# A mark for weights of ones on the softmax sums, with a simpler order of the loop

## The chip, the cores and the metric

The kernel runs on one core of a Trainium2 chip. The metric is the device time of one execution, in microseconds. The core's engines have a queue of instructions each and wait for one another by semaphores: TensorE (PE in the profile, its weight loads PEld), VectorE (DVE), ScalarE (ACT), GpSimd (POOL), and SyncE (SP), which issues most of the transfers.

## What is computed

A block of three layers on x of shape (2, 256, 128, 128), that is batch, time, bands, channels, all in float32: attention over time with a causal mask, attention over the bands with a mask of |i - j| <= 16, and a feed-forward layer, each after a layer norm and each added to its input. There are 4 heads of 32 channels.

```
xt = _ln(x, ln_t_w, ln_t_b).transpose(0, 2, 1, 3)
x = x + _mha(xt, t_wi, t_bi, t_wo, t_bo, H_T, cm).transpose(0, 2, 1, 3)
xf = _ln(x, ln_f_w, ln_f_b)
x = x + _mha(xf, f_wi, f_bi, f_wo, f_bo, H_F, bm)
xn = _ln(x, ln_n_w, ln_n_b)
h = jax.nn.gelu(xn @ w1.T + b1, approximate=False)
x = x + (h @ w2.T + b2)
```

In `_mha` the scores are `q k / sqrt(32)` plus the mask, `attn` their softmax over the keys, and the output `(attn v) wo.T + bo`.

## The kernel before

The work is cut into 384 groups of 512 rows of 128 channels, NT = 4 tiles of 128 rows. First come 128 groups of attention over time (`OverTime`, two sequences of 256 steps each), then 32 rounds of four groups of attention over bands (`OverBands`, four sequences of 128 bands each) and four feed-forward groups (`FeedForward`) on the same rows. The class `Attention` holds what the two attentions share.

A group goes through stages, each a method that emits the instructions of one step:

- `load` issues the transfer of the input (for several groups at once).
- `statistics` makes mean and variance on VectorE (`stats`, `mv`) and 1/sqrt on GpSimd (`rstd`, two instructions).
- `normalize` makes `xh` on VectorE, four instructions.
- `transpose` has four transposes on TensorE into `xp`, and `take_transposed` copies them to `xnT` on VectorE.
- `queries_keys` and `values` are the projections `qp`, `kp` and `vp`; `take_query`, `take_key` and `take_values` copy them out, on ScalarE but for the key over time, which VectorE takes.
- `first_half` and `second_half` make scores `sp` on TensorE, each head on 32 rows of the array; `first_function` and `second_function` take their exponential on ScalarE (`pt`, `pf`) and clear what the mask excludes, on GpSimd, and for head 3 over bands by a product with a band of ones on VectorE.
- `weigh` sums the weights over the keys by a product with ones (`rp`, each head's sums on its own 32 columns of the array) and multiplies them with the values (`op`). There is no maximum taken out: a test at the start of the program shows that the scores are small enough.
- `invert` makes 1/rp on ScalarE as exp(-ln(rp)), and `divide` refines it and divides on VectorE: `t`, `u`, `oT`. `divide_alone` does the same with VectorE's reciprocal.
- `bias` adds the output's bias to the residual, on GpSimd.
- `output` is the last projection `yp`, and `finish` adds it to the residual on VectorE and issues the store, where there is one.

A feed-forward group uses the same names: its halves are two hidden products `hp` each, its functions two GELUs into `hT`, its `weigh` the second product `zp` and its `divide` the addition to the residual and the store.

Every engine keeps the order in which the program emits (`keep_in_program_order`), so the loop in `run` (lines 878 to 923) sets the order of all five engines by hand. Step n emits the scores of group n, the weighing of group n - 1, and the projections of group n + 1. `near(n, far, name)` calls a stage for a group 2 ahead if it is attention and 1 ahead if it is feed-forward (`AHEAD`), with `far` more. The loop before has three orders: one for the first feed-forward group after bands (all hidden products at once, `divide_alone`), one for the second, and one for all else. In it the output of group n - 2 stands at the start of step n, all four heads' scores over bands are made in `first_half`, and the transposes of a feed-forward group come ahead of the second pair of hidden products.

ScalarE needs one table of functions for exp and ln and another for GELU, so the loop changes tables twice a round. All PSUM tiles come from one pool of eight banks, taken in turn. All products are float32 on both sides.

In the profile nearly all lines are L798, that of the helper `pinned` that emits; groups are told apart by tile names.

Of the kernel before, what the change touches and what calls it, by code (L numbers as in the profile page):

```python
# [9 lines left out]
F32 = mybir.dt.float32  # L10
# [3 lines left out]
ALU = mybir.AluOpType  # L14
# [4 lines left out]
P = 128  # L19
H = 4  # L20
D = 32
# [3 lines left out]
NT = 4  # L25
# [4 lines left out]
EXP_SET = "natural_log_exp_and_others"  # L30
# [393 lines left out]
class Group:  # L424
# [58 lines left out]
    def second_half(self):  # L483
        pass

    def second_function(self):
        pass
# [32 lines left out]
class Attention(Group):  # L520
# [57 lines left out]
        self.oT = path.work.tile([P, NT * P], F32, name="oT", bufs=2)  # L578
        vector.scalar_tensor_tensor(self.oT, t, 2.0, u, ALU.subtract, ALU.mult)

    def divide_alone(self):

        path, vector = self.path, self.path.vector
        r = path.work.tile([P, NT * P], F32, name="r", bufs=2)
        vector.reciprocal(r, self.rp)
        self.oT = path.work.tile([P, NT * P], F32, name="oT", bufs=2)
        vector.scalar_tensor_tensor(self.oT, self.op, -1.0, r, ALU.mult, ALU.mult)

    def output(self):
        path = self.path  # L590
        self.yp = path.bank([P, NT, P], "yp")
# [11 lines left out]
def rows_of(h):  # L603
    return slice(h * D, (h + 1) * D)


class OverTime(Attention):
# [4 lines left out]
    W = 3 * P  # L612
# [45 lines left out]
    def weigh(self):  # L658
        path = self.path
        p, v, W = self.p, self.v, self.W  # L660
        rp = path.bank([P, 2, 2 * P], "rp")
        one = path.k.ones[:, 0:D]
        for h in range(H):
            path.tensor.matmul(rp[rows_of(h), :, :], one, p[:, :, h, 0 : 2 * P], start=True, stop=False)
        for h in range(H):
            path.tensor.matmul(rp[rows_of(h), :, P : 2 * P], one, p[:, :, h, 2 * P : W], start=False, stop=True)
        op = path.bank([P, 2, 2 * P], "op")
        for s in range(2):
            for h in range(H):
                r = rows_of(h)  # L670
                path.tensor.matmul(op[r, s, :], v[:, 2 * s, r], p[:, s, h, 0 : 2 * P], start=True, stop=False)
            for h in range(H):
                r = rows_of(h)
                path.tensor.matmul(
                    op[r, s, P : 2 * P], v[:, 2 * s + 1, r], p[:, s, h, 2 * P : W], start=False, stop=True
                )
        self.op = op.rearrange("p s q -> p (s q)")
        self.rp = rp.rearrange("p s q -> p (s q)")


class OverBands(Attention):
# [32 lines left out]

    def first_half(self):
        self.p = self.path.work.tile([P, H, NT, P], F32, name="pf", tag="p")
        self.scores(range(H))

    def first_function(self):
        self.weights(range(H))  # L720

    def weigh(self):
        path = self.path
        self.rp = path.bank([P, NT * P], "rp")
        for h in range(H):
            path.tensor.matmul(
                self.rp[rows_of(h), :], path.k.ones[:, 0:D], self.p[:, h].rearrange("p i q -> p (i q)"),
                start=True, stop=True,
            )
        self.op = path.bank([P, NT * P], "op")  # L730
        for i in range(NT):
            c = slice(i * P, (i + 1) * P)
            for h in range(H):
                r = rows_of(h)
                path.tensor.matmul(self.op[r, c], self.v[:, i, r], self.p[:, h, i, :], start=True, stop=True)
# [67 lines left out]
class BoundedPath:  # L803
# [19 lines left out]
    def bank(self, shape, name):  # L823
        return self.ps.tile(shape, F32, name=name, tag="ps")

    def groups(self, x, out):
        nc, k = self.nc, self.k
        B, T, FB, C = x.shape
        NC_T = T // P
        S = NT // NC_T  # L830
        for b in range(B):
            xv = x[b].rearrange("(o p) f c -> p o f c", p=P)
            x1v = k.x1[b].rearrange("(o p) f c -> p o f c", p=P)
            for f0 in range(0, FB, GA):
                held = {}

                def load(f0=f0, xv=xv, held=held):
                    held["x"] = self.xpool.tile([P, GA, NC_T, C], F32, name="xt", tag="x")
                    for o in range(NC_T):
                        nc.sync.dma_start(held["x"][:, :, o, :], xv[:, o, f0 : f0 + GA, :])  # L840

                for g in range(0, GA, S):

                    def src(g=g, held=held):
                        return held["x"][:, g : g + S].rearrange("p f o c -> p (f o) c")

                    def store(t, f=f0 + g, x1v=x1v):
                        for o in range(NC_T):
                            nc.sync.dma_start(
                                x1v[:, o, f : f + S, :],  # L850
                                t.rearrange("p (f o) c -> p f o c", o=NC_T)[:, :, o, :],
                            )

                    yield OverTime(self, src, None, load if g == 0 else None, store)
        for b in range(B):
            x1v = k.x1[b].rearrange("t f c -> f t c")
            outv = out[b].rearrange("t f c -> f t c")
            for t0 in range(0, T, GB):
                held = {}

                def load(t0=t0, x1v=x1v, held=held):
                    held["x"] = self.xpool.tile([P, GB, C], F32, name="xb", tag="x")
                    nc.sync.dma_start(held["x"], x1v[:, t0 : t0 + GB, :])
                    held["x2"] = self.xpool.tile([P, GB, C], F32, name="x2", tag="x2", bufs=2)

                def part(name, g, held=held):
                    return lambda: held[name][:, g : g + NT, :]

                for g in range(0, GB, NT):
                    yield OverBands(self, part("x", g), part("x2", g), load if g == 0 else None)  # L870
                for g in range(0, GB, NT):

                    def store(t, g=t0 + g, outv=outv):
                        nc.sync.dma_start(outv[:, g : g + NT, :], t)

                    yield FeedForward(self, part("x2", g), None, None, store)

    def run(self, x, out):
        groups = list(self.groups(x, out))

        def do(n, *names):
            if 0 <= n < len(groups):
                for name in names:
                    getattr(groups[n], name)()

        def near(n, far, name):

            for d in (1, 2):
                if 0 <= n + d + far < len(groups) and groups[n + d + far].AHEAD == d:
                    do(n + d + far, name)  # L890

        def at(n, kind):
            return 0 <= n < len(groups) and isinstance(groups[n], kind)

        def move(n):
            near(n, 0, "transpose")
            near(n, 0, "take_transposed")

        self.scalar.preload_act_table_set(EXP_SET)
        for n in range(-7, len(groups) + 2):  # L900
            feeding = [at(n - i, FeedForward) for i in range(3)]
            do(n + 7, "load")
            near(n, 0, "normalize")
            if feeding[0] and at(n - 1, OverBands):

                do(n, "first_half", "first_function", "second_half", "second_function")
                do(n - 2, "output", "finish")
                near(n, 1, "statistics")
                move(n)
                do(n, "bias")  # L910
                do(n - 1, "weigh", "divide_alone")
            elif feeding[1] and at(n - 2, OverBands):
                do(n, "first_half", "first_function", "bias")
                do(n - 1, "weigh", "divide")
                move(n)
                do(n - 2, "output", "finish")
                near(n, 1, "statistics")
                do(n, "second_half", "second_function")
            else:
                do(n - 2, "output", "finish")  # L920
                near(n, 1, "statistics")
                if feeding[1] and at(n, OverBands):
                    self.scalar.preload_act_table_set(EXP_SET)
                do(n, "first_half", "first_function", "bias")
                early = at(n, OverBands) and at(n + 1, FeedForward)
                if early:
                    move(n)
                do(n - 1, "weigh", "invert", "divide")
                if feeding[0] and at(n + 1, FeedForward):
                    move(n)  # L930
                    early = True
                do(n, "second_half", "second_function")
                do(n + 1, "queries_keys", "take_query", "take_key", "values", "take_values")
                if not early:
                    move(n)


def bounded_path(tc, k, x, out):
# [66 lines left out]
```

## Time and profile before

| | us |
|---|---|
| median of 3 runs | 3130.95 (3130.63 to 3132.49) |
| the profiled execution | 3130.63 |
| its span, first to last instruction | 3128.7 |
| a step of the stage over time (128 of them) | 8.59 |
| a round of four band and four feed-forward groups (32) | 62.2 |

Granted clock of TensorE: 0.999 in the profiled execution. The stage over time takes the first 1,140 us or so of the span, and the rounds take the rest. In one round TensorE is busy 59.4 us, VectorE 45.6, GpSimd 37.4 and ScalarE 32.4. A product's time in the profile is that of its record, which overlaps the next one's; what it costs TensorE is the distance from its start to the start of the next.

### The profile page before, as it was taken

What the parts mean: (1) busy time and instruction counts of PE and PEld (TensorE: products, weight loads), DVE (VectorE), ACT (ScalarE), POOL (GpSimd) and SP (SyncE); (2) the same over time, 40 slices, a digit from 0 to 9 for tenths busy, and PEclk for the clock granted to TensorE, in tenths of its full rate; (3) what the DMA queues carried; (4) which work ended last, traced back from release to release, by engine and by line L of the source; (5) the groups of instructions that cost most, each with busy time, mean ns of one, the idle gap of its engine ahead of it and who ended that gap; (6) DMA issues with size and microseconds to landing.
All of it is one profiled execution on the core that took longest, in us unless ns stands there. A gap on an engine that the chain in (4) does not pass through costs nothing.

```text
span 3128.7 us, 77496 instructions
## 1 busy us (share of the span) xinstructions
PE 3013.3 (96%) x31270; PEld 2133.5 (68%) x31270; DVE 2246.7 (72%) x6414; ACT 1748.6 (56%) x3200; POOL 1889.3 (60%) x2441
## 2 busy tenths in 40 slices
PE   7999999999999999999999999999999999999998
PEld 5666666666666666666666666666666666776676
DVE  6776767777677677677767767776777677767775
ACT  4666666666666664554455445544554555455544
POOL 4666666666666665566556656665665566556654
PEclk9999999999999999999999999999999999999999
DMA  3222222222222221101111111111101110111000
GB/s 84 59 59 72 59 59 60 71 59 61 72 61 59 59 62 35 35 28 43 34 35 28 45 35 32 28 45 35 32 28 45 35 32 28 45 35 32 28 22 22
DMA packets 222863, 140.55 MB, mean 45 GB/s; under 512 B 7968, under 2 KB 205984, under 8 KB 222496
## 3 DMA queue, kind: packets, MB, share of 16 engines
q1 hardware_dynamic: 221248, 134.45, 15.3%
q8 instruction: 249, 4.08, 0.5%
q10 hardware_dynamic: 1248, 1.05, 0.1%
q14 instruction: 118, 0.97, 0.1%
HBM read 68.36 MB, written 67.11 MB: 43 GB/s over the span
## 4 chain that ended last, share of the span: by engine, by line
PE 80%; DVE 13%; ACT 5%; issue 1%; DMA 0%; POOL 0%; SPq 0%; ACTq 0%; POOLq 0%; DVEq 0%
PE zp L798 15%; PE hp L798 15%; PE sp L798 10%; PE yp L798 7%; PE rp L798 7%; PE qp L798 6%; PE op L798 6%; PE vp L798 5%; PE kp L798 5%; PE xp L798 4%; DVE xh L798 3%; ACT pf L798 3%; DVE stats L798 2%; DVE oT L798 2%; DVE t L798 1%; DVE x L798 1%
## 5 line engine op out<-in xcount | busy, mean ns | idle before, releaser
L798 POOL TENSOR_SCALAR rstd<-mv 128x4 f32<-128x4 f32 x384 | 99.2, 258 | 1131.9 <-DVE mv L798 1131.9
L798 ACT ACTIVATE hT<-hp,b 128x512 f32<-128x512 f32 x512 | 351.9, 687 | 620.8 <-PE hp L798 616.4
L798 ACT ACTIVATE pt<-sp 128x384 f32<-128x384 f32 x1024 | 419.3, 496 | 303.6 <-PE sp L798 303.6
L798 POOL TENSOR_SCALAR_AFFINE_SELECT pf<-pf 128x512 f32<-128x512 f32 x768 | 533.9, 711 | 38.6 <-ACT pf L798 12.3
L798 PEld LDWEIGHTS zp<-w2T_sb,hT 128*128 128x128 f32 x4096 | 475.0, 192 | 50.4 <-issue 38.7
L798 PE MATMUL hp<-xnT,w1f 128*128 128x512 f32 x1024 | 471.5, 598 | 34.0 <-DVE xnT L798 34.0
L798 PE MATMUL zp<-w2T_sb,hT 128*128 128x128 f32 x4096 | 481.5, 276 | 0.1
L798 DVE COPY xnT<-xp 128x512 f32<-128x512 f32 x384 | 260.0, 684 | 278.9 <-PE xp L798 278.9
L798 POOL TENSOR_TENSOR rstd<-rstd,mhalf 128x4 f32<-128x4 f32 x384 | 399.7, 1041 | 32.0
L798 PE MATMUL sp<-qT,kT 32*128 32x128 f32 (+1 forms) x8192 | 389.4, 315 | 0.0
L798 ACT ACTIVATE pf<-sp 128x512 f32<-128x512 f32 x512 | 264.4, 602 | 202.9 <-PE sp L798 202.6
L798 PEld LDWEIGHTS sp<-qT,kT 32*128 32x128 f32 x8192 | 310.8, 185 | 64.6 <-issue 35.9
L798 PEld LDWEIGHTS vp<-wf,xnT 128*128 128x128 f32 x2048 | 269.1, 192 | 123.0 <-issue 85.5
L798 PEld LDWEIGHTS hp<-xnT,w1f 128*128 128x128 f32 x1024 | 181.9, 190 | 218.6 <-issue 162.4
L798 PE MATMUL yp<-wn,oT 128*128 128x128 f32 x2048 | 275.1, 277 | 46.8 <-DVE oT L798 46.8
L798 POOL TENSOR_SCALAR_AFFINE_SELECT pt<-pt 128x512 f32<-128x512 f32 x512 | 314.4, 636 | 0.0
L798 PEld LDWEIGHTS yp<-wn,oT 128*128 128x128 f32 x2048 | 251.1, 192 | 73.9 <-ACT v L798 58.6
L798 PE MATMUL qp<-xnT,wf 128*128 128x512 f32 x512 | 282.7, 634 | 1.2 <-DVE xnT L798 1.2
L798 DVE TENSOR_TENSOR t<-rp,r 128x512 f32<-128x512 f32 x224 | 154.5, 690 | 174.8 <-ACT r L798 173.9
L798 PE MATMUL vp<-wf,xnT 128*128 128x128 f32 x2048 | 269.9, 275 | 0.0
L798 DVE TENSOR_SCALAR xh<-x,mv,rstd 128x128 f32<-128x128 f32 x512 | 256.3, 562 | 15.1 <-POOL rstd L798 15.1
L798 PE MATMUL kp<-xnT,wf 128*128 128x512 f32 x512 | 262.3, 594 | 0.0
(94 smaller groups left out, 4630.5 us busy)
## 6 DMA issues: line engine op xcount, KB each, us to landing
xt<-in_x SPq DMA_DIRECT2D x64, 512.0 KB, 5.5
x<-rd SPq DMA_DIRECT2D x256, 128.0 KB, 1.9
out<-res SPq DMA_DIRECT2D x128, 256.0 KB, 2.3
xb<-x SPq DMA_DIRECT2D x32, 0.5 KB, 6.1
w1T_sb<-in_w1T ACTq DMA_DIRECT2D x1, 256.0 KB, 3.8
w2T_sb<-in_w2T ACTq DMA_DIRECT2D x1, 256.0 KB, 4.2
t_wiT_sb<-in_t_wiT ACTq DMA_DIRECT2D x1, 192.0 KB, 2.5
f_wiT_sb<-in_f_wiT ACTq DMA_DIRECT2D x1, 192.0 KB, 3.9
```

Source lines behind the costliest of these rows:

```text
L798: return self.tc.keep_in_program_order(emit(*args, **kwargs))
```

## The change

The edit has two parts. A new method `sums` emits the products with ones as raw instructions with the mark `is_weight_onezero`, for both attentions; the place on the array is given outright and is the one they had. And the loop is replaced by one with a single order: `output` and `finish` of group n - 1 stand at the end of step n, the transposes just ahead of them, and `statistics` ahead of `normalize`. The band groups' scores and exponentials are made in two halves of two heads, the second after the weighing of the group before. `divide_alone` is gone; at the first feed-forward group after bands (`turn`) the GELUs of the first half wait until the last band group's `invert` has been emitted.

```diff
-    def divide_alone(self):
-        path, vector = self.path, self.path.vector
-        r = path.work.tile([P, NT * P], F32, name="r", bufs=2)
-        vector.reciprocal(r, self.rp)
-        self.oT = path.work.tile([P, NT * P], F32, name="oT", bufs=2)
-        vector.scalar_tensor_tensor(self.oT, self.op, -1.0, r, ALU.mult, ALU.mult)
...
-        one = path.k.ones[:, 0:D]
         for h in range(H):
-            path.tensor.matmul(rp[rows_of(h), :, :], one, p[:, :, h, 0 : 2 * P], start=True, stop=False)
+            path.sums(h, rp[rows_of(h), :, :], p[:, :, h, 0 : 2 * P], True, False)
         for h in range(H):
-            path.tensor.matmul(rp[rows_of(h), :, P : 2 * P], one, p[:, :, h, 2 * P : W], start=False, stop=True)
+            path.sums(h, rp[rows_of(h), :, P : 2 * P], p[:, :, h, 2 * P : W], False, True)
...
     def first_half(self):
         self.p = self.path.work.tile([P, H, NT, P], F32, name="pf", tag="p")
-        self.scores(range(H))
+        self.scores((0, 1))
     def first_function(self):
-        self.weights(range(H))
+        self.weights((0, 1))
+    def second_half(self):
+        self.scores((2, 3))
+    def second_function(self):
+        self.weights((2, 3))
...
+    def sums(self, h, out, p, start, stop):
+        tensor = self.nc.tensor
+        ins = tensor.add_instruction(
+            mybir.InstMatmult(
+                name=self.nc.get_next_instruction_name(),
+                ins=[tensor.lower_ap(p), tensor.lower_ap(self.k.ones[:, 0:D])],
+                outs=[tensor.lower_ap(out)],
+                start_tensor_calc=start, stop_tensor_calc=stop, is_weight_onezero=True,
+                tile_size=(P, D), tile_position=(0, h * D),
+            )
+        )
+        self.tc.keep_in_program_order(ins)
...
-        for n in range(-7, len(groups) + 2):
-            feeding = [at(n - i, FeedForward) for i in range(3)]
-            do(n + 7, "load")
-            near(n, 0, "normalize")
-            if feeding[0] and at(n - 1, OverBands):
-                do(n, "first_half", "first_function", "second_half", "second_function")
-                do(n - 2, "output", "finish")
-                near(n, 1, "statistics")
-                move(n)
-                do(n, "bias")
-                do(n - 1, "weigh", "divide_alone")
-            elif feeding[1] and at(n - 2, OverBands):
-                do(n, "first_half", "first_function", "bias")
-                do(n - 1, "weigh", "divide")
-                move(n)
-                do(n - 2, "output", "finish")
-                near(n, 1, "statistics")
-                do(n, "second_half", "second_function")
-            else:
-                do(n - 2, "output", "finish")
-                near(n, 1, "statistics")
-                if feeding[1] and at(n, OverBands):
-                    self.scalar.preload_act_table_set(EXP_SET)
-                do(n, "first_half", "first_function", "bias")
-                early = at(n, OverBands) and at(n + 1, FeedForward)
-                if early:
-                    move(n)
-                do(n - 1, "weigh", "invert", "divide")
-                if feeding[0] and at(n + 1, FeedForward):
-                    move(n)
-                    early = True
-                do(n, "second_half", "second_function")
-                do(n + 1, "queries_keys", "take_query", "take_key", "values", "take_values")
-                if not early:
-                    move(n)
+        for n in range(-7, len(groups) + 2):
+            turn = at(n, FeedForward) and at(n - 1, OverBands)
+            if at(n, OverBands) and at(n - 1, FeedForward):
+                self.scalar.preload_act_table_set(EXP_SET)
+            do(n + 7, "load")
+            near(n, 1, "statistics")
+            near(n, 0, "normalize")
+            do(n, "first_half")
+            if not turn:
+                do(n, "first_function")
+            do(n, "bias")
+            do(n - 1, "weigh", "invert", "divide")
+            if turn:
+                do(n, "first_function")
+            do(n, "second_half", "second_function")
+            do(n + 1, "queries_keys", "take_query", "take_key", "values", "take_values")
+            near(n, 0, "transpose")
+            near(n, 0, "take_transposed")
+            do(n - 1, "output", "finish")
```

(`move(n)` in the old loop is `transpose` and `take_transposed` of `near(n, 0)`.)

More of the change, by code (lines that the diff above doesn't have):

```diff
@@ L725, in weigh @@
         for h in range(H):
[L726 to L729, printed above, removed]
+            path.sums(h, self.rp[rows_of(h), :], self.p[:, h].rearrange("p i q -> p (i q)"), True, True)
         self.op = path.bank([P, NT * P], "op")
@@ L893, in at @@
             return 0 <= n < len(groups) and isinstance(groups[n], kind)
-        def move(n):
+        self.scalar.preload_act_table_set(EXP_SET)
+        for n in range(-7, len(groups) + 2):
+            turn = at(n, FeedForward) and at(n - 1, OverBands)
+            if at(n, OverBands) and at(n - 1, FeedForward):
+                self.scalar.preload_act_table_set(EXP_SET)
+            do(n + 7, "load")
[10 more added lines that the diff above has]
+            do(n + 1, "queries_keys", "take_query", "take_key", "values", "take_values")
@@ L896, in move @@
             near(n, 0, "transpose")
             near(n, 0, "take_transposed")
-        self.scalar.preload_act_table_set(EXP_SET)
-        for n in range(-7, len(groups) + 2):
-            feeding = [at(n - i, FeedForward) for i in range(3)]
-            do(n + 7, "load")
-            near(n, 0, "normalize")
-            if feeding[0] and at(n - 1, OverBands):
-                do(n, "first_half", "first_function", "second_half", "second_function")
-                do(n - 2, "output", "finish")
-                near(n, 1, "statistics")
-                move(n)
-                do(n, "bias")
-                do(n - 1, "weigh", "divide_alone")
-            elif feeding[1] and at(n - 2, OverBands):
-                do(n, "first_half", "first_function", "bias")
-                do(n - 1, "weigh", "divide")
-                move(n)
-                do(n - 2, "output", "finish")
-                near(n, 1, "statistics")
-                do(n, "second_half", "second_function")
-            else:
-                do(n - 2, "output", "finish")
-                near(n, 1, "statistics")
-                if feeding[1] and at(n, OverBands):
-                    self.scalar.preload_act_table_set(EXP_SET)
-                do(n, "first_half", "first_function", "bias")
-                early = at(n, OverBands) and at(n + 1, FeedForward)
-                if early:
-                    move(n)
-                do(n - 1, "weigh", "invert", "divide")
-                if feeding[0] and at(n + 1, FeedForward):
-                    move(n)
-                    early = True
-                do(n, "second_half", "second_function")
-                do(n + 1, "queries_keys", "take_query", "take_key", "values", "take_values")
-                if not early:
-                    move(n)
```

## The prediction

> **What bounds the kernel now.** I read the page from the top: the share of each engine, then the chain that ended last.
>
> ```profile
> span 3128.7 us, 77496 instructions
> ...
> PE 3013.3 (96%) x31270; PEld 2133.5 (68%) x31270; DVE 2246.7 (72%) x6414; ACT 1748.6 (56%) x3200; POOL 1889.3 (60%) x2441
> ...
> PE 80%; DVE 13%; ACT 5%; issue 1%; DMA 0%; POOL 0%; SPq 0%; ACTq 0%; POOLq 0%; DVEq 0%
> ```
>
> TensorE is busy 96% of the span and is 80% of the chain; no other engine is near. So the sum to make is TensorE's: what its products take from start to start, and where it waits. Next the groups of instructions with shapes kept apart, on TensorE.
>
> ```profile
> L798 PE MATMUL sp<-qT,kT 32*128 32x128 f32 x6144 | 252.5, 278 | 0.0
> ...
> L798 PE MATMUL xp<-ident,xh 128*128 128x128 f32 x1536 | 234.7, 275 | 20.5 <-DVE xh L798 20.5
> ...
> L798 PE MATMUL rp<-pf,ones 128*32 128x512 f32 x1024 | 137.3, 605 | 0.0
> L798 PE MATMUL rp<-pt,ones 128*32 128x512 f32 x1024 | 136.4, 605 | 1.5 <-POOL pt L798 1.5
> ...
> L798 PE MATMUL rp<-pt,ones 128*32 128x256 f32 x1024 | 78.7, 379 | 0.0
> ```
>
> Counts matter here. 128 band groups issue 4 sums each, 512 products, and the row has 1,024: a float32 product leaves two records. The transposes `xp` have 384 x 4 = 1,536 records, one each. Also 6,144 x 278 ns of `sp` fit into 252.5 us busy: the four heads, on 32 rows each, run side by side. Then the timeline of TensorE, first in the stage over time (start, duration, what).
>
> ```profile
> 563.28 1.06 PE L798 MATMUL yp<-wn,oT 128*128 128x128 f32 x8
> 564.27 0.94 PE L798 MATMUL sp<-qT,kT 32*128 32x256 f32 x16
> 565.13 1.50 PE L798 MATMUL rp<-pt,ones 128*32 128x512 f32 x16
> 566.45 1.48 PE L798 MATMUL op<-pt,v 128*32 128x256 f32 x32
> 567.86 0.94 PE L798 MATMUL sp<-qT,kT 32*128 32x256 f32 x16
> 568.73 1.12 PE L798 MATMUL qp<-xnT,wf 128*128 128x512 f32 x2
> ```
>
> No idle time is marked; a step is 572.86 - 564.27 = 8.59 us, and the sums hold 565.13 to 566.45, 1.32 us. Last, one period of four band groups and four feed-forward groups (62.2 us, from 1595.7 to 1657.9).
>
> ```profile
> 1644.20 1.13 PE L798 MATMUL yp<-wn,oT 128*128 128x128 f32 x8 [0.66 <-DVE oT L798]
> 1645.26 1.17 PE L798 MATMUL sp<-qT,kT 32*128 32x128 f32 x32
> 1646.37 1.06 PE L798 MATMUL rp<-pf,ones 128*32 128x512 f32 x8
> 1647.25 1.06 PE L798 MATMUL op<-pf,v 128*32 128x128 f32 x32
> ...
> 1651.91 1.13 PE L798 MATMUL yp<-wn,oT 128*128 128x128 f32 x8 [0.80 <-DVE oT L798]
> ...
> 1654.93 0.33 PE L798 MATMUL xp<-ident,xh 128*128 128x128 f32 x1 [0.31 <-DVE xh L798]
> ...
> 1657.89 2.41 PE L798 MATMUL hp<-xnT,w1f 128*128 128x512 f32 x5 [0.76 <-DVE xnT L798]
> ```
>
> TensorE's waits here are 0.66, 0.80, 0.31, 0.76 and one of 0.30 earlier in the period: 2.8 us. The four-head score product takes 1.11 us and the sums 0.88 us, start to start.
>
> **What the Trainium skill says.** *FP8 and Floating Point Precision*, "TensorE Precision Notes": true float32 takes four passes, high and low part of each operand. Ones have no low part, so half the passes can go. The trace agrees with two records of two passes: a record of 512 columns holds the array 0.43 us (2 x 512 columns), and it has no product with the mark. *TensorE: Matmul & The Clock Gate*, Part 3 and "Why this matters for your kernels": products on different 32-row groups run at once, and a product on 32 rows alone is no shorter than one on 128. It agrees: eight 128-column records of `sp` per head in 1.11 us for four heads, eight of `vp` on the whole array in 0.89. *TensorEngine Tiling (Array Packing)*, "Key Properties": changing the tiling mode drains the array. The 1.11 against 0.89 is such an entry and exit, 0.2 us. *SBUF — State Buffer*, "Who interferes with whom": VectorE with two SBUF inputs and GpSimd block one another; the band product took 0.69 us mostly and 1.12 once, beside GpSimd's masks, so it agrees.
>
> **Part 1, the mark.** If each marked product leaves one record, the stage over time keeps one of two rounds of 512 columns and one of two of 256: 1.32 us becomes 0.45 + 0.22 = 0.67, saving 0.65 a step. Does TensorE stay the bound at 7.94 us? By windows, VectorE is busy 774.6 us in the 1,100 us of the stage, 6.0 us a step; GpSimd 5.4, ScalarE 5.6. The one chain that tightens is ln, r, t, u, oT: in the trace oT ends 5.84 us after the step's first score product (570.11), and the output product starts at 571.88; with the mark it wants it 0.65 sooner, at 571.23. A slack of 1.1 us is left. ln gains nothing, it waits for ScalarE's exponentials of the first half anyway. The order of the other products in this stage is the same in both loops: the output moves from the head of a step to the tail of the one before. Statistics come before the normalization now, which only helps GpSimd. Saving: 128 x 0.65 = 83 us. Bounds: zero (no effect) to 128 x 1.0 = 125 (a quarter of the passes; the transposes, one record each, still take 0.11 us per 128 columns, so I take half). In the band groups 0.88 becomes 0.45: 4 x 0.43 = 1.7 us a period.
>
> **Part 2, scores of the band groups in two halves.** Two heads have the same eight rounds as four: 0.21 us for the first, six of 0.11, 0.22 to the next product, 1.10 us. So two halves cost 2.20 where 1.11 was: 1.1 us more a group, 4.4 a period. Bounds: 0.86 a half if entry and exit vanished (2 x 0.86 less 1.11 is 0.6 a group, 2.5 a period), to 1.2 (5.2 a period). I take 4.4, plus 0.1 since the query product of the first band group now follows a score product. The gain of Part 1 in these groups is thus overpaid.
>
> **Part 3, the order around the turn.** I lay TensorE's new order out with the old durations. An inner band step is sp 1.10, rp 0.45, op 0.99, sp 1.10, q/k/v 2.71, xp 0.44, yp 1.0: 7.8 us. ScalarE does two exponentials (to 2.2 us), ln and r (to 3.5); VectorE t, u, oT to 5.55, since the band product of head 3 now comes after. The output product is asked for at 6.35 or later: the 0.66 and 0.80 go. What is late instead:
> - third to fourth band step: GpSimd's queue is rstd (after statistics, which wait for the finish of the step before), four masks of 0.7, bias 1.3, two masks. Statistics end at 2.0 us, so 2.0 + 1.3 + 2.8 + 1.3 + 1.4 = 8.9; that step is only 7.35 long (no transposes), and the sums ask at 7.35 + 1.10. Wait 0.45.
> - fourth band step: no queries of a next group, so the output product follows the transposes at 4.5 us but oT ends at 5.65: 1.25. `xnT` of the first feed-forward group is behind oT and the band product: 0.15.
> - first feed-forward step: the sums of the fourth band group wait for its last mask, 0.25; the output product for oT behind ln, r, t and u, 0.55. The 3.35 us reciprocal of `divide_alone` goes, but VectorE had room there.
> - feed-forward steps: transposes are now the last product of a step and the next begins with hidden products that need their copy. From the last row's start 0.63 + 0.68 + 0.07 us, less 0.44 on TensorE: 0.95 for the third group, 0.5 for the fourth, where a second set of transposes covers part.
> The table load moves behind ln and r; GELU of the first group ends at 8.5 us and its second product is asked for at 9.3, so it is hidden. The moved DMA issues (stores of `finish`) are SP's, whose DMA share is 0.12 here; they come half a step earlier and nobody waits for them.
>
> Waits: 0.45 + 1.25 + 0.15 + 0.25 + 0.55 + 0.95 + 0.5 = 4.1 us in place of 2.8 (3.6 counted start to start, with the drained tails). The period: 62.2 - 3.6 + 4.5 - 1.7 + 4.1 + 0.2 for drained tails = 65.7, 3.5 us more; 32 periods, 110 us.
>
> Sum: +110 - 83 = +27 us. The profiled execution took 3130.63 us (its span 3128.7 and 1.9 around it) and the median of three is 3130.95, so the same frame serves: 3158 us.
>
> **The rivals.**
> - Waits at the turn shorter: the sum of waits stays at the 2.8 that TensorE shows now. For it: four of my seven waits hang on one chain (masks, sums, logarithm, division), and half a microsecond found in it counts twice. Against it: the 0.95 and 0.5 for `xnT` don't hang on it. Price 1.3 x 32 = 42: 3116, faster. It decides below 3.2 us of waits; under 3.0 the gain exceeds 0.2%.
> - A quarter of the passes stays: 128 x (0.32 + 0.21) = 68 us more saved, 3090. Against: the transposes.
> - The mark does nothing: 83 + 55 back, 3296. For: nothing shows a marked product. Against: one record for a transpose, two for all else.
> - GpSimd becomes the bound of the band steps: its masks stretched from 3.9 to 4.8 us per six in the period shown; with the scores in halves they also start later. At 0.5 us in each of four steps, 2.0 x 32 = 64: 3222.
>
> **How the numbers follow.** My forecast 0.60, waits shorter 0.15, a quarter 0.05, no effect 0.06, GpSimd 0.14. Within 0.2% (6 us) counts as no change, about what this measurement can tell. Slower: 0.9 of the forecast's 0.60, GpSimd and no effect, 0.74. Faster: 0.8 of the short waits, the quarter, 0.03 of the forecast: 0.19. Same: 0.07. The range takes the waits down to 2.4 us (3105) and GpSimd up to most of its price (3215); the quarter, no effect and the ends of the rest lie outside. The forecast alone has 3135 to 3190.
>
> **What would show it.** `rp` rows with 1,024 + 512 records in place of 3,072, and an over-time step of 7.94 us, show Part 1. Two `sp` entries of 16 records, each about 1.1 us to the next product, show Part 2; 0.55 each would make it wrong by 4 x 32 x 1.1 = 140 us. In Part 3 the waits of `hp` for `xnT` should be the largest in feed-forward steps and `yp` for `oT` near 1.25 once a period. The prediction is wrong in sign if a period comes out under 64.8 us.

## The result and the profile after

The changed kernel takes 3305.34 us (median of 4 runs, 3304.5 to 3305.86), the kernel before 3131.2 beside it: a ratio of 1.0555, 95% interval 1.0537 to 1.0574. It is slower by 174 us. The forecast had the sign, but 27 us, and the result lies outside its range of 3105 to 3215.

From the page of the changed kernel, the lines that answer to those of before:

```profile
span 3303.2 us, 77870 instructions
...
PE 3183.6 (96%) x31270; PEld 2258.3 (68%) x31270; DVE 2192.1 (66%) x6446; ACT 1803.9 (55%) x3264; POOL 1845.2 (56%) x2441
...
PE 89%; DVE 7%; ACT 2%; issue 1%; DMA 0%; POOL 0%; SPq 0%; ACTq 0%; DVEq 0%
```

TensorE is as full as before, with the same 31,270 records, but they cover 170 us more. A mark that removed half the passes of the sums would have left 1,536 records fewer. The groups on TensorE by shape (count, busy us, mean ns, idle before) say the same of the changed rows:

```profile
L792 PE MATMUL sp<-qT,kT 32*128 32x128 f32 x6144 | 399.3, 278 | 0.0
...
L823 PE MATMUL rp<-pf,ones 128*32 128x512 f32 x1024 | 155.8, 605 | 0.0
...
L823 PE MATMUL rp<-pt,ones 128*32 128x512 f32 x1024 | 136.4, 605 | 0.5 <-POOL pt L792 0.5
...
L823 PE MATMUL rp<-pt,ones 128*32 128x256 f32 x1024 | 78.7, 379 | 0.0
```

The sums still leave 3,072 records of the same 605 and 379 ns. The band scores, with the same 6,144 records of the same 278 ns, now cover 399.3 us in place of 252.5: they overlap less. The timeline of TensorE in the stage over time is unchanged:

```profile
563.01 0.94 PE L792 MATMUL sp<-qT,kT 32*128 32x256 f32 x16
...
571.61 0.94 PE L792 MATMUL sp<-qT,kT 32*128 32x256 f32 x16
572.47 1.50 PE L823 MATMUL rp<-pt,ones 128*32 128x512 f32 x16
573.78 1.48 PE L792 MATMUL op<-pt,v 128*32 128x256 f32 x32
```

The sums hold 572.47 to 573.78, 1.31 us, and a step is 571.61 - 563.01 = 8.60 us, as before. So all of the 174 us is in the rounds. Between the first sums of two rounds lie 67.69 us in place of 62.21, and 32 x 5.48 = 175 us. Counted from start to start without the marked waits, the scores of a round hold TensorE 8.72 us in place of 4.41: 4.3 of the 5.5 us. The places of a round where TensorE waits:

```profile
1700.20 1.16 PE L792 MATMUL sp<-qT,kT 32*128 32x128 f32 x16
1701.29 0.66 PE L792 MATMUL xp<-ident,xh 128*128 128x128 f32 x4
1702.92 1.13 PE L792 MATMUL yp<-wn,oT 128*128 128x128 f32 x8 [0.97 <-DVE oT L792]
1704.56 1.96 PE L792 MATMUL hp<-xnT,w1f 128*128 128x512 f32 x4 [0.51 <-DVE xnT L792]
...
1711.11 1.13 PE L792 MATMUL yp<-wn,oT 128*128 128x128 f32 x8 [0.37 <-DVE oT L792]
...
1720.47 1.98 PE L792 MATMUL hp<-xnT,w1f 128*128 128x512 f32 x4 [0.79 <-DVE xnT L792]
...
1728.96 1.98 PE L792 MATMUL hp<-xnT,w1f 128*128 128x512 f32 x4 [0.35 <-DVE xnT L792]
```

A half of the scores, 16 records, takes 1700.20 to 1701.29, 1.09 us; all four heads together took 1.11 before. The waits stand where the forecast's list has them, 2.99 us in place of its 3.4 (one of them, 0.51, is well over its 0.15); that is hardly more than the 2.8 of before. One wait is not marked as idle, since other products slip in. In the fourth band step of the next round:

```profile
1765.42 1.25 PE L823 MATMUL rp<-pf,ones 128*32 128x512 f32 x6
1766.30 0.39 PE L792 MATMUL op<-pf,v 128*32 128x128 f32 x4
1766.50 0.60 PE L823 MATMUL rp<-pf,ones 128*32 128x512 f32 x2
1766.52 1.45 PE L792 MATMUL op<-pf,v 128*32 128x128 f32 x28
1767.90 1.16 PE L792 MATMUL sp<-qT,kT 32*128 32x128 f32 x16
```

The sums of one head come late, and sums and `op` take 1767.90 - 1765.42 = 2.48 us where a band step without it has 0.88 + 0.99 = 1.87. That is the forecast's wait for GpSimd's last mask (0.45), at 0.6 us.

### The profile page after: what moved, and what is told of

Same layout as the page of the kernel before. It is cut to its first block, busy times and chain, and to the rows that moved or that the text cites. A ratio compares the mean times of both kernels' runs of the same rounds, so it can differ in the third digit from the quotient of the medians.

```text
span 3303.2 us, 77870 instructions
## 1 busy us (share of the span) xinstructions
PE 3183.6 (96%) x31270; PEld 2258.3 (68%) x31270; DVE 2192.1 (66%) x6446; ACT 1803.9 (55%) x3264; POOL 1845.2 (56%) x2441
## 4 chain that ended last, share of the span: by engine, by line
PE 89%; DVE 7%; ACT 2%; issue 1%; DMA 0%; POOL 0%; SPq 0%; ACTq 0%; DVEq 0%
PE sp L792 14%; PE zp L792 14%; PE hp L792 12%; PE rp L823 10%; PE qp L792 8%; PE vp L792 7%; PE op L792 7%; PE kp L792 7%; PE yp L792 6%; PE xp L792 4%; DVE xnT L792 2%; DVE oT L792 1%; DVE t L792 1%; ACT r L792 1%; DVE u L792 1%; ACT ln L792 1%
## 5 line engine op out<-in xcount | busy, mean ns | idle before, releaser
L792 POOL TENSOR_SCALAR rstd<-mv 128x4 f32<-128x4 f32 x384 | 88.3, 230 | 1224.3 <-DVE mv L792 1222.7
L792 ACT ACTIVATE hT<-hp,b 128x512 f32<-128x512 f32 x512 | 341.3, 687 | 514.5 <-PE hp L792 510.7
L792 POOL TENSOR_SCALAR_AFFINE_SELECT pf<-pf 128x512 f32<-128x512 f32 x768 | 546.6, 720 | 100.1 <-ACT pf L792 73.8
L792 PE MATMUL hp<-xnT,w1f 128*128 128x512 f32 x1024 | 493.9, 605 | 52.9 <-DVE xnT L792 52.9
L792 PE MATMUL sp<-qT,kT 32*128 32x128 f32 (+1 forms) x8192 | 536.2, 315 | 0.0
L792 PEld LDWEIGHTS sp<-qT,kT 32*128 32x128 f32 x8192 | 433.2, 185 | 87.6 <-issue 55.1
L792 ACT ACTIVATE pf<-sp 128x512 f32<-128x512 f32 x512 | 278.0, 595 | 306.0 <-PE sp L792 294.1
L792 DVE TENSOR_TENSOR t<-rp,r 128x512 f32<-128x512 f32 x256 | 177.0, 692 | 314.8 <-ACT r L792 312.3
L792 DVE SCALAR_TENSOR_TENSOR oT<-t,u 128x512 f32<-128x512 f32 x256 | 273.2, 1067 | 8.8
L792 DVE TENSOR_TENSOR res<-zp,res 128x512 f32<-128x512 f32 x128 | 88.5, 692 | 268.3 <-issue 141.9
```

Source lines behind the costliest of these rows:

```text
L792: return self.tc.keep_in_program_order(emit(*args, **kwargs))
```

## Experiments: does the mark do anything?

The theory after the result: the mark takes no pass away, and the loop alone makes the difference.

**The changed kernel without the mark.**

```diff
-                start_tensor_calc=start, stop_tensor_calc=stop, is_weight_onezero=True,
+                start_tensor_calc=start, stop_tensor_calc=stop,
```

> The changed kernel with the mark left out of its raw products, all else kept. Theory (the mark takes no pass away): 3305 us as the changed kernel has, within 6 us, and the same 3,072 records of the sums. Rival (the mark works in part, or itself costs something, say an order of the loads that is lost): the time differs from 3305 us by more than 6 us, upwards if the mark helped at all.

Measured: 3305.14 us (3304.12 to 3306.03), 3,072 records of the sums, a round of 67.68 us. The mark makes no difference in the changed loop.

**The mark without the new loop.** The kernel before with `sums` for both attentions, and the mark on the one product of the tests at the start, whose weights are ones on the whole array.

```diff
-            path.tensor.matmul(rp[rows_of(h), :, :], one, p[:, :, h, 0 : 2 * P], start=True, stop=False)
+            path.sums(h, rp[rows_of(h), :, :], p[:, :, h, 0 : 2 * P], True, False)
...
-        nc.tensor.matmul(tp, k.ones, tests, start=True, stop=True)
+        marked(nc, tp, k.ones, tests, is_weight_onezero=True)
```

> The kernel before with the marked sums alone, its loop kept, and the mark also on the one product with ones on the whole array, that of the tests at the start. Theory: 3131 us within 6 us, 3,072 records of the sums, and 2 records of the product of the tests as before. Rival (the mark works, and the loop lost more than its gain): about 3131 - 138 = 2993 us with 1,536 records. Second rival (the mark works on the whole array alone, and is dropped on a tile of 32 columns): 3131 us, but 1 record of the product of the tests.

Measured: 3130.57 us, a ratio of 1.0001 (0.9992 to 1.001). Its groups on TensorE by shape:

```profile
L836 PE MATMUL rp<-pf,ones 128*32 128x512 f32 x1024 | 137.3, 605 | 0.0
L836 PE MATMUL rp<-pt,ones 128*32 128x512 f32 x1024 | 136.4, 605 | 1.5 <-POOL pt L805 1.5
L836 PE MATMUL rp<-pt,ones 128*32 128x256 f32 x1024 | 78.7, 379 | 0.0
...
L335 PE MATMUL tp<-tests,ones 128*128 128x6 f32 x2 | 0.6, 370 | 1.5 <-DVE tests L399 1.5
```

One product `tp`, marked, on the whole array, still leaves two records. It isn't the tile of 32 columns that loses the mark. So the mark alone costs and gains nothing, and the loop alone makes the 174 us. Whether TensorE ignores the mark, or it is lost on the way from the program to TensorE, no run here shows.

**The transposes as marked products.** In the forecast the transposes, one record each, stood for "an operand of zeros and ones takes half". Here they are ordinary products with the identity, marked on the moving side.

```diff
-            path.tensor.transpose(self.xp[:, i * P : (i + 1) * P], self.xh[:, i, :], path.k.ident)
+            marked(path.nc, path.tc, self.xp[:, i * P : (i + 1) * P], self.xh[:, i, :], path.k.ident, is_fmap_onezero=True)
```

> The kernel before, with its transposes issued as ordinary products with the identity that carry the mark for a moving side of zeros and ones, in place of the transpose instruction (the order is kept). Theory (no such mark takes passes away here): 3,072 records of xp in place of 1,536, each group 0.43 us more on TensorE, at most 384 x 0.43 = 165 us in all, so 3240 to 3300 us. Rival (the mark works on the moving side, or on the whole array): 1,536 records and 3131 us.

Measured: 3263.26 us (two runs, ratio 1.0423, 1.0402 to 1.0444), a step over time of 9.05 us in place of 8.59. The row of its transposes:

```profile
L335 PE MATMUL xp<-ident,xh 128*128 128x128 f32 x3072 | 411.1, 278 | 10.6 <-DVE xh L810 10.6
```

3,072 records: the same operands take two records as a product and one as a transpose. The saving belongs to the transpose instruction, not to the zeros and ones.

## Experiments: what half the passes would have been worth

**Two bfloat16 products for one float32 product.** A record of the float32 sums holds the array 0.43 us for 512 columns; two bfloat16 products together take about that. The upper half of a float32 word is a bfloat16 number, so no copy is needed. The lower 16 bits of each weight are left out of the sum.

```diff
+        top = p.bitcast(BF16)[:, :, :, 1 : 2 * W : 2]
...
+        for i in range(2):
+            self.tensor.matmul(out, self.k.half, p, start=start and i == 0, stop=stop and i == 1)
```

> The changed kernel with the sums made in two bfloat16 products of the upper halves of the weights with 0.5 each, in place of one float32 product; the lower 16 bits of each weight are left out of the sum. It takes the array time that a float32 product with half its passes would. Theory (all of the forecast but the mark was right): 8.59 - 0.65 = 7.94 us a step over time, 65.7 us a round, 3158 us, up to 3170 since the measured round lies 0.3 us over the forecast's sum. Rival (the order costs more than was laid out and was covered by the longer sums, or VectorE and ScalarE hold the stage over time above 8.3 us a step): over 3200 us.

Measured: 3190.99 us (3185.7 to 3194.86), ratio 1.0196 (1.0179 to 1.0213). Its timeline on TensorE:

```profile
572.40 0.94 PE L795 MATMUL sp<-qT,kT 32*128 32x256 f32 x16
573.26 0.87 PE L795 MATMUL rp<-pt,half 128*32 128x512 bf16 x16
573.96 1.48 PE L795 MATMUL op<-pt,v 128*32 128x256 f32 x32
```

The sums hold 0.70 us and a step 7.97, as laid out (0.67 and 7.94): no other engine stops the stage over time. A round is 66.49 us, 0.8 more than laid out. The time lies between the theory (up to 3170) and the rival (over 3200): the stage over time came as laid out, the rounds did not. Of four shorter sums a round, three came through, 0.88 us to 0.46 each. The fourth did not, in the fourth band step:

```profile
1738.64 0.63 PE L795 MATMUL rp<-pf,half 128*32 128x512 bf16 x4
1739.66 0.41 PE L795 MATMUL rp<-pf,half 128*32 128x512 bf16 x2 [0.39 <-POOL pf L795]
...
1741.10 1.16 PE L795 MATMUL sp<-qT,kT 32*128 32x128 f32 x16
```

Sums and `op` take 2.46 us here, 2.48 with the float32 sums: GpSimd's last mask ends this step's sums either way.

**The same in the loop before.**

```diff
-            path.tensor.matmul(rp[rows_of(h), :, :], one, p[:, :, h, 0 : 2 * P], start=True, stop=False)
+            for i in range(2):
+                path.tensor.matmul(rp[rows_of(h), :, :], one, top[:, :, h, 0 : 2 * P], start=i == 0, stop=False)
```

> The kernel before, its loop kept, with the sums in two bfloat16 products of the upper halves of the weights with 0.5; the lower 16 bits of each weight are left out of the sum. It shows what half the passes would be worth without the new loop. Theory (in the rounds the waits for VectorE grow by what the sums lose, as with one pass): 7.97 us a step over time, 62.2 to 62.4 us a round, 3131 - 128 x 0.62 = 3051 us. Rival (TensorE still holds the rounds at half the sums): 60.5 us a round, 2997 us.

Measured: 3051.88 us, ratio 0.975 (0.9734 to 0.9766), 7.97 us a step, 62.21 us a round, as the theory had it. In the loop before, the shorter band sums bring nothing at all.

**One bfloat16 product.** The sums are one product of the upper halves with ones; the lower 16 bits are left out of the sum.

```diff
-        one = path.k.ones[:, 0:D]
+        one = path.k.ones_b
+        top = p.bitcast(BF16)[:, :, :, 1 : 2 * W : 2]
```

> The kernel before with the sums as one bfloat16 product of the upper halves of the weights with ones; the lower 16 bits of each weight are left out of the sum. Theory: the sums over time fall from 1.32 to about 0.43 us a step, 128 x 0.89 = 114 us; in the rounds the output product waits for the division in two of the three inner band steps already, so little of 4 x 0.56 us a round comes through: 0.8 us, 26 us. 2991 us. Rival (all of the shorter sums come through): 2945 us. Second rival (another engine holds the stage over time at 8 us or more): 3050 us.

Measured: 3024.12 us, ratio 0.9659 (0.9643 to 0.9675). The step over time falls to 7.72 us; a round takes 62.40 on average. Even the 26 us that the expectation left to the rounds didn't come. Where they went, on TensorE's timeline of one round:

```profile
1658.74 1.13 PE L802 MATMUL yp<-wn,oT 128*128 128x128 f32 x8 [1.32 <-DVE oT L802]
...
1666.44 1.13 PE L802 MATMUL yp<-wn,oT 128*128 128x128 f32 x8 [1.46 <-DVE oT L802]
...
1672.42 3.70 PE L802 MATMUL hp<-xnT,w1f 128*128 128x512 f32 x8 [1.42 <-DVE xnT L802]
...
1679.65 1.96 PE L802 MATMUL hp<-xnT,w1f 128*128 128x512 f32 x4 [0.94 <-DVE xnT L802]
```

Before, the same four waits are 0.66, 0.80, 0.76 and 0.30 us: each has grown by 0.64 to 0.66 us, by all that a sum lost (0.88 to 0.24). Each sum of a round is followed by a wait for VectorE, whose chain doesn't begin earlier when the sums end earlier. For the two output products it begins with four exponentials on ScalarE, which the logarithm stands behind. For the two hidden products it is the copy `xnT`, which stands in VectorE's queue behind the addition of the last `yp` and the statistics. The 62.40 is an average: most rounds take 62.21, as before, and three take about 1.7 us more (the last section shows one).

**One product over time alone.** The band groups keep their float32 sums (the edit is against the kernel just above).

```diff
-                self.rp[rows_of(h), :], path.k.ones_b,
-                self.p[:, h].rearrange("p i q -> p (i q)").bitcast(BF16)[:, 1 : 2 * NT * P : 2],
+                self.rp[rows_of(h), :], path.k.ones[:, 0:D], self.p[:, h].rearrange("p i q -> p (i q)"),
```

> The kernel before with the sums as one bfloat16 product of the upper halves of the weights in the stage over time alone; the lower 16 bits of each weight are left out of the sum there, and the band groups keep their float32 sums. Theory (a shorter sum is worth nothing in the rounds of the old loop): 7.72 us a step, 62.2 us a round, 3019 us, no more than with both (3024). Rival (the band sums did bring something): 3030 us or more.

Measured: 3019.75 us, ratio 0.9647 (0.9631 to 0.9663), 7.72 us a step and 62.21 a round. It is the fastest version here, ahead of both kernels, but its sums over time leave out the lower bits.

## Experiments: the halves and the order

**The halves put back together in the changed loop, and the halves alone in the loop before.** The two kernels make the table of two by two.

```diff
-        self.scores((0, 1))
+        self.scores(range(H))
```

> The changed kernel with the band scores of all four heads in the first half again. Theory (two heads take the array as long as four, 1.10 us): 128 x 1.1 = 141 us less than 3305, so 3164 us, give or take 20 for waits that shift, since the exponentials of all heads come ahead of the logarithm again. Rival (the halves cost nothing and the order of the loop costs all): 3305 us, or more.

> The kernel before with the band scores in two halves and nothing else. Theory: 141 us of score products more, less what the waits for the output product give back (0.66 and 0.80 us in three steps of a round, at most 70 us in all): 3200 to 3272 us. Rival (halves are hidden or half as long): within 20 us of 3131.

| us (a round) | four heads at once | two halves |
|---|---|---|
| loop before | 3130 (62.21) | 3228.34 (65.26) |
| changed loop | 3274.04 (66.72) | 3305.34 (67.69) |

The first expectation missed: whole scores gain 31 us in the changed loop, not 141. The second held: halves cost 98 us in the loop before. The new order with whole scores costs 144 us, so the two parts of the loop cost less together (174) than the sum of each alone. The score products themselves are about 1.1 us a group apart in both loops, so the rest is waits, and in the changed loop the clock. In the loop before with halves the marked waits of TensorE fall from 2.8 to 1.1 us a round: the output products no longer wait. In the changed loop with whole scores they rise from 3.0 to 5.9, and the largest is in the fourth band step:

```profile
1689.08 0.66 PE L786 MATMUL xp<-ident,xh 128*128 128x128 f32 x4
...
1692.76 1.48 PE L786 MATMUL yp<-wn,oT 128*128 128x128 f32 x8 [3.02 <-DVE oT L786]
1694.03 3.26 PE L786 MATMUL hp<-xnT,w1f 128*128 128x512 f32 x4
...
1760.19 1.13 PE L786 MATMUL yp<-wn,oT 128*128 128x128 f32 x8 [3.02 <-DVE oT L786]
1761.16 1.88 PE L786 MATMUL hp<-xnT,w1f 128*128 128x512 f32 x4
```

With all exponentials ahead of the logarithm, `oT` is later, and this step has neither a second half of scores nor projections to fill the time. The second half was cover for a wait as well as a cost. The lines show two rounds. In the first the four hidden products took 3.26 us after the wait, in the second 1.88 after the same wait. The first kind came in 18 of 32 rounds. From one such wait to the next it is 67.4 us after the slow products and 65.75 after the fast ones, so about 1.0 us of the average round is the slow products, and whole scores gain 1.9 us where they don't occur.

**Transposes of feed-forward steps behind the second product again.**

```diff
+            early = at(n, FeedForward) and not turn and at(n + 1, FeedForward)
+            if early:
+                near(n, 0, "transpose")
+                near(n, 0, "take_transposed")
             do(n, "second_half", "second_function")
...
-            near(n, 0, "transpose")
-            near(n, 0, "take_transposed")
+            if not early:
+                near(n, 0, "transpose")
+                near(n, 0, "take_transposed")
```

> The changed kernel with the transposes and their copies of the second and third feed-forward step put behind the second product again, ahead of the second pair of hidden products. Theory: the waits of hp for xnT of 0.79 and 0.35 us a round go, with the drains ahead of them 1.4 us, 32 x 1.4 = 45 us: 3260 us. Rival (the copy then waits in VectorE's queue and the wait only moves): 3290 us or more.

Measured: 3251.46 us, 54 us under the changed kernel, a round of 66.03. The waits of 0.79 and 0.35 are gone, and the marked waits of a round fall from 3.0 to 1.8 us; the round gains 1.66, a little more than the theory's 1.4.

**The third band group's output behind the first hidden products.**

```diff
-            near(n, 1, "statistics")
+            if not turn:
+                near(n, 1, "statistics")
             near(n, 0, "normalize")
             do(n, "first_half")
+            if turn:
+                do(n - 2, "output", "finish")
+                near(n, 1, "statistics")
...
-            do(n - 1, "output", "finish")
+            if not (at(n, OverBands) and at(n + 1, FeedForward)):
+                do(n - 1, "output", "finish")
```

> The changed kernel with one output moved back: that of the third band group of a round stands after the first hidden products of the first feed-forward group, with its finish and the statistics that need it. Theory: the waits of yp for oT of 0.97 and of hp for xnT of 0.51 us a round go, some of it to the sums of the fourth band group, which wait for GpSimd's masks then; 32 x 1.0 to 32 x 1.6, so 3254 to 3273 us. Rival (the masks of the fourth band group take the place of the whole wait): 3300 us or more.

Measured: 3396.62 us. The theory failed; the number falls under the rival's "3300 or more", but not by the rival's cause, for the long wait is not one for the masks. The timeline at the turn (TensorE and VectorE):

```profile
1724.94 0.69 DVE L792 SCALAR_TENSOR_TENSOR oT<-t,u 128x512 f32<-128x512 f32 x1
1725.55 1.12 DVE L792 TENSOR_TENSOR pf<-pf,band 128x512 f32<-128x512 f32 x1
1726.59 0.68 DVE L792 COPY xnT<-xp 128x512 f32<-128x512 f32 x1
...
1727.32 3.18 PE L792 MATMUL hp<-xnT,w1f 128*128 128x512 f32 x4 [2.52 <-DVE xnT L792]
1730.30 1.58 PE L792 MATMUL yp<-wn,oT 128*128 128x128 f32 x8
```

The hidden products need `xnT`, and its copy stands in VectorE's queue behind `oT` and the band product. So the output product had been filling a wait that is there anyway; taken out, the two waits became one of 2.52 us, and the output costs its full time later. Then, in this round, the hidden products ran at 3.18 us in place of 1.96. The windows of this stretch (from:to, length, busy time and count of each engine, granted clock, DMA share, GB/s):

```profile
1718.00:1724.00 6.00, 6.00 (x87) 4.69 (x85) 3.95 (x15) 3.31 (x6) 5.28 (x8) 1.00 0.02 4
1724.00:1728.00 4.00, 1.48 (x10) 0.88 (x9) 3.97 (x7) 1.09 (x2) 3.93 (x5) 1.00 0.00 0
1727.30:1730.30 3.00, 2.98 (x5) 1.20 (x6) 2.12 (x4) 0.00 (x0) 1.72 (x3) 0.61 0.30 76
1730.30:1731.80 1.50, 1.50 (x9) 1.38 (x7) 0.00 (x0) 0.00 (x0) 0.00 (x0) 0.64 1.03 336
1732.00:1736.00 4.00, 4.00 (x48) 2.09 (x40) 3.42 (x12) 2.92 (x4) 2.04 (x3) 1.00 0.26 69
```

After the wait the granted clock was 0.61 and 0.64 for some four microseconds, and 1.00 again after. Such slow products follow the wait in 23 of 32 rounds. A round without them takes 69.22 us, 1.5 more than the changed kernel's; the average is 70.7, so about half of the loss is the clock. The transfer that runs beside them is not the cause: in a round where the hidden products after the same wait took 1.82 us to the next product, it ran too, at a DMA share of 0.90 with the clock at 1.00 (from 1660 to 1662).

**Both moves.** The late output and the early transposes in one kernel.

> The changed kernel with the late output and the early feed-forward transposes together. Theory (the two are independent and add): the sum of the two gains, 3200 to 3222 us, which would bring it level with or under the kernel before with half scores (3228). Rival (the second only takes over what the first freed): no more than 15 us under the better one of the two.

Measured: 3364.66 us (69.57 us a round). The theory's number fell with the run before it. Against the late output alone the early transposes give 32 us here and 54 without it, but that doesn't show that the two moves depend on one another: here the products after the wait of 2.52 us were slow in all 32 rounds. They took about 2.1 us a round more than at the full clock, against 1.6 with the late output alone. Without that the two rounds would be some 1.7 us apart (an estimate from these figures), about the 1.66 of the early transposes alone.

## Why the prediction was wrong

- **Part 1, the mark: this step failed.** It put the gain at 0.65 us a step and 1.7 us a round, since ones have no low part, and took "one record for a transpose" as the sign that zeros and ones halve a float32 product; measured, the gain is zero. The marked transposes show that the transpose instruction does that; both marks, on weights and on the moving side, take nothing away. The rival "the mark does nothing", worked out at 3296 us and given 0.06, is what happened, 9 us under the measured time. The sign was right all the same, since the forecast had the loop cost more than the mark could give.
- The value of half the passes over time, 0.65 us a step and no other engine in the way, was right: 0.62 measured with two bfloat16 passes. In the rounds it was mis-sized: 1.7 us was taken and 67.69 - 66.49 = 1.2 us came, since with short sums the wait for GpSimd's last mask was 1.0 us (1738.64 to 1739.66) and not the 0.45 laid out. The chain behind that 0.45 adds up to 8.8, not 8.9; the mask ended 9.4 us into the step, with masks and `bias` longer than the sum had them (2.96 and 1.70 us for 2.8 and 1.3).
- **Part 2, the halves:** 1.10 us each was right (1.09). The 4.4 us a round is right for the products. It isn't what undoing the halves brings, 1.0 us a round in the changed loop, because waits and the clock change with it. That the 0.2 us a half beyond the streaming is the entry into and exit from the tiling mode is a reading that no run here tests.
- **Part 3, the order:** the places were right: `yp` for `oT` at 0.97 and 0.37 (1.25 and 0.55 forecast), `hp` for `xnT` at 0.51, 0.79 and 0.35 (0.15, 0.95, 0.5), and the late mask at 0.6 with the long sums (0.45, laid out for short ones). The wait of 0.25 for the fourth group's sums isn't there: the hidden products ended after the mask. A round without the mark's 1.7 us comes to 67.4 by the prediction's terms, and 67.69 was measured. Part of this closeness is luck: the waits, 3.6 us in all with the late mask, are 0.5 under the forecast's 4.1, and the rest of the round is 0.8 over it. The forecast took 0.8 us off for the drained tails of the old waits and put 0.2 on for those of the new; measured, the products other than the scores take 0.4 us a round more than before, not less.
- With the passes really halved the same kernel takes 3191 us: within the range, 33 us over the forecast. 25 of them are the round's 66.49 against 65.7, and 16 of these 25 are the 0.5 us a round of the mis-sized band sums; some 4 are the step of 7.97. The rest is the spread of its runs: these figures are from the execution of 3185.7 us, 5 under the median.
- The prediction priced the mark only in the changed loop. In the loop before, half the passes bring 79 us, all over time. With half the passes the new loop stays 60 us above the kernel before, so it would have spent more than the mark could give, even if the mark had worked. Of the loop's cost, 54 us are the places of two transposes; the rest is halves and order together, and the other single moves are not tried apart.

## What to carry to other kernels

Before pricing a flag by an instruction that seems to use it, ask whether that instruction is another one; the count of records in one small product tells whether the flag does anything. Shortening a product is worth its time only in steps where the next wait isn't set by another engine: four waits here grew by all that the sums lost. A product on the critical engine can be cover for a wait, so undoing a costly one may return a fraction of its price.

## What was not expected of the hardware

A wait of TensorE can cost more than itself, and not each time. After the wait of 2.52 us in the kernel with the late output the products were slow in 23 of 32 rounds, after the 3.02 us with whole scores in 18 of 32, mostly every other round. A shorter wait doesn't exclude it: in the kernel with one bfloat16 product, three rounds have this in place of 3.70 us, and the granted clock was 0.51 over the first 1.8 us of it:

```profile
1297.19 5.39 PE L802 MATMUL hp<-xnT,w1f 128*128 128x512 f32 x8 [1.42 <-DVE xnT L802]
```

It also occurs once in the changed kernel with two bfloat16 products, after waits of 1.37 and 0.74 us. In the rounds of both compared kernels, where no wait is over 0.98 us, it doesn't occur. So the length of one wait alone doesn't decide; what does stays open. The Trainium skill, *TensorE: Matmul & The Clock Gate*, in "Why this matters for your kernels", asks for no idle gaps over about 3 us between bursts of matmuls; here the clock fell after marked waits of 2.52 and 1.42 us too.
